# A macaron transformer block on one core: a first weight load in halves, five tiles' V copies on GpSimd, and the last block stored tile by tile from two queues

## The chip, the cores and the metric

The kernel runs on one core of a Trainium2 chip. The metric is the device time of one execution in microseconds (us); lower is better. The engines are named as in the profile: PE (TensorE matmuls), PEld (its weight loads), DVE (VectorE), ACT (ScalarE), POOL (GpSimd) and SP (SyncE, which here only issues DMAs). "SPq" and "ACTq" are the queues of SP and ACT, from which DMAs are issued.

## The reference, cut to what matters

The input is `x` of 2 x 2048 tokens with 256 features. The block is a feed-forward half, a local attention and a second feed-forward half with the same weights:

```python
x = x + 0.5 * ffn(layernorm(x))      # routed experts + shared expert
x = x + attn(layernorm(x))           # 16 heads of 16, causal within groups of 64 tokens
x = x + 0.5 * ffn(layernorm(x))

def ffn(x):                          # 4096 tokens x 256
    # top 2 of 8 experts, at most 640 tokens an expert, weights from a softmax
    routed = scatter_add(expert_e(tokens of e) * weight)     # expert: silu(x@rg) * (x@ru) @ rd, inner 1024
    shared = silu(x @ sg) * (x @ su) @ sd                    # inner 2048
    return shared + routed

def attn(x):                         # x: groups of 64 tokens
    q, k, v = split(x @ w_qkv); q, k = rmsnorm(q) * ln_w, rmsnorm(k) * ln_w
    return softmax(mask(q @ k.T / 4)) @ v @ w_proj
```

## The kernel before

Tokens are taken in 8 blocks of 512 (BT), a block in 4 tiles of 128 (P). Every fp32 operand of a large product is split into a high and a low fp16 part, and a product is three matmuls (`TERMS`: high x high, high x low, low x high). Four phases follow each other:

- **Phase a** normalises tiles, computes routing and runs the shared expert of blocks 0 to 3. The shared weights are loaded once at the start: `load_shared` (L124) goes over the 16 inner chunks in pairs, loads gate and up rows of a pair into a raw tile `rs` (tag `raw`, two DMAs), the down rows into `rd` (one DMA), and splits them into `sgu` and `sdw` (`split`, L104: ACT makes the high part, L107, DVE the low part, L109). The pair c = 0 is issued from ACT's queue, the others from SP's. The first product of the kernel, L398, waits for chunk 0 of `sgu`; it also needs the turned tiles `xb` (L200 to L202).
- **Phase b** runs the eight routed experts of the first half.
- **Phase c** runs the attention in 32 tiles (`attn_tile`, L625), beside the shared expert of the remaining blocks of the first half (4 to 7) and of the first seven blocks of the second half.
- **Phase d** runs the routed experts of the second half and then the shared expert of block 7, whose end is the end of the kernel.

The shared expert of a block (`shared`, L454) goes over 16 chunks c. `gate_up` (L385) makes gate and up in PSUM (tiles `pgu`, three buffers, 12 matmuls of 512 columns at L408), then SiLU (ACT L420; in phase c a tanh on ACT L416 and a DVE step L417 instead), the product with up (DVE L422), the high part `hh` (ACT L424) and the low part `hl` (DVE L425). `down` (L428) multiplies them with the down weights into two PSUM tiles `po` (12 matmuls of 256 columns, L435). It runs one chunk late: `defer` (L99) holds back a chunk's `down` until the next chunk's `gate_up` has been traced. In the very last chunk (block 7, c = 15) gate and up are made in two halves of 256 tokens, and `down` takes the tiles in pairs (0, 1) and (2, 3). Then `fin` adds the sums to the residual `xr` (DVE L472, one instruction for two tiles) and stores 256 KB at a time from SP (L475).

An attention tile projects q, k and v (`pqk` and `pv`, L768), splits v into `vs` (one buffer; ACT L658, DVE L659), normalises q and k (L651 to L664) and spreads them into `QK` (L674 to L681), transposes `QK` by DMA (L686), multiplies (`psc`, L694), adds the mask (DVE L697), takes the maximum (L703) and subtracts it (POOL L704). Then `vs` is copied into `V2`, a layout for pairs of heads: four copies of 64 x 512 fp16 (ACT L709). The exponential (ACT L713), its high part (ACT L715), its low part (POOL L716), a DMA transpose (L719), the product with V2 (`py`, L727), the division (L739 to L744) and the output projection (`pao`) follow. V2 has two buffers, taken in turn.

What order the instructions take on each engine is set when the program is built: the framework's scheduler issues, in a simulated time line, the instruction that comes first in the program's order among those that are ready. Two things bend that order: Python generators, which interleave the tracing of tiles with the tracing of chunks (`drive`, `run_slots`), and `tc.issue_after(ins)`, which puts what it encloses behind `ins` on that instruction's engine. On the chip every engine then runs its own list in order.

Of the kernel before, what the change touches and what calls it, by code (L numbers as in the profile page):

```python
# [15 lines left out]
ALU = mybir.AluOpType  # L16
# [4 lines left out]
P = 128  # L21
H = 256
# [3 lines left out]
WS = 16.0  # L26
XP = UP * WS
NB = 8
BT = 512
# [8 lines left out]
class Net:  # L38
# [85 lines left out]
    def load_shared(self, sg, su, sd):  # L124

        nc = self.nc
        w = self.wsh
        self.sgu = w.tile([P, 16, 2, 2, 2, P], F16, name="sgu")
        self.sdw = w.tile([P, 2, 16, H], F16, name="sdw")
        for c in range(0, 16, 2):  # L130
            issue = nc.sync if c else nc.scalar
            r = self.raw.tile([P, 2, 2, 2 * P], F32, name=f"rs{c}", tag="raw", bufs=4)
            for i, s in enumerate((sg, su)):
                issue.dma_start(
                    out=r[:, i], in_=s[:, c * P:(c + 2) * P].rearrange("(k p) f -> p k f", p=P))
            r2 = self.raw.tile([P, 2, H], F32, name=f"rd{c}", tag="raw2", bufs=4)
            issue.dma_start(out=r2, in_=sd[c * P:(c + 2) * P].rearrange("(k p) f -> p k f", p=P))
            if c == 0:
                yield
            for j in range(2):  # L140
                with self.behind(True, 0, 1, mark=self.turned[1] if c + j == 0 else None):
                    src = r[:, :, :, j * P:(j + 1) * P]
                    self.split(self.sgu[:, c + j, 0], self.sgu[:, c + j, 1], src, None if c + j else self.normal[3])
            with self.behind(True, 0, 1):
                self.split(self.sdw[:, 0, c:c + 2], self.sdw[:, 1, c:c + 2], r2)
            yield
# [238 lines left out]
    def gate_up(self, wc, x, h, tanh=False, first=False):  # L385


        nc = self.nc
        n = x.shape[-1]
        ps = []  # L390
        if first:
            ps = [self.ps_gu.tile([P, n], F32, name="pgu", tag="gu") for _ in range(2)]
            for half in range(2):
                t = slice(half * n // 2, (half + 1) * n // 2)
                for j, (w, a) in enumerate(TERMS):
                    for i in range(2):
                        for k in range(2):
                            nc.tensor.matmul(  # L398
                                ps[i][:, t], lhsT=wc[:, w, i, k, :], rhs=x[:, 2 * a + k, t],
                                start=(half == 0 and j + k == 0), stop=(half == 1 and j + k == 3),  # L400
                                skip_group_check=True)
        for i in range(2):
            if not first:
                p = self.ps_gu.tile([P, n], F32, name="pgu", tag="gu")
                j = 0
                for k in range(2):
                    for (w, a) in TERMS:
                        nc.tensor.matmul(  # L408
                            p, lhsT=wc[:, w, i, k, :], rhs=x[:, 2 * a + k, :], start=(j == 0), stop=(j == 5))
                        j += 1  # L410
                ps.append(p)
            p = ps[i]
            if i == 0:
                s = self.hp.tile([P, BT], F32, name="sl")[:, :n]
                if tanh:
                    nc.scalar.activation(s, p, AF.Tanh, scale=0.5 / XP)  # L416
                    nc.vector.scalar_tensor_tensor(  # L417
                        out=s, in0=s, scalar=1.0, in1=p, op0=ALU.add, op1=ALU.mult)
                else:
                    self.latest[0] = nc.scalar.activation(s, p, AF.Silu, scale=1.0 / XP).ins  # L420
                yield
        self.latest[1] = nc.vector.scalar_tensor_tensor(  # L422
            out=s, in0=ps[1], scalar=1.0 / XP / (2.0 * XP if tanh else 1.0), in1=s, op0=ALU.mult, op1=ALU.mult).ins
        self.highs.append(nc.scalar.copy(h[0], s).ins)  # L424
        self.lows.append(nc.vector.tensor_tensor(out=h[1], in0=s, in1=h[0], op=ALU.subtract).ins)  # L425
        yield
# [27 lines left out]
    def shared(self, b, xb, src, dst, tanh=False, late=2, last=False):  # L454
        nc = self.nc
        outs = [self.ps_out.tile([P, BT], F32, name="po", tag="po") for _ in range(2)]
        for c in range(16):
            if c == late:
                res = self.res_load(src, b)
            h = [a[:, 0:BT] for a in self.hbuf()]  # L460
            if last and c == 15:
                for t in (slice(0, BT // 2), slice(BT // 2, BT)):
                    yield from self.gate_up(self.sgu[:, c], xb[:, :, t], [a[:, t] for a in h], tanh)
            else:
                yield from self.gate_up(self.sgu[:, c], xb, h, tanh, b == 0 and c == 0 and not tanh)

            def fin(c=c, h=h):
                self.down(outs, 4, h, self.sdw[:, :, c], c, 16, last and c == 15)
                if c < 15:
                    return  # L470
                for i in range(2):
                    nc.vector.scalar_tensor_tensor(  # L472
                        out=res[i], in0=outs[i].rearrange("p (t f) -> p t f", f=H), scalar=0.5 / WS,
                        in1=res[i], op0=ALU.mult, op1=ALU.add)
                    nc.sync.dma_start(  # L475
                        out=dst[b * BT + i * 2 * P:b * BT + (i + 1) * 2 * P].rearrange("(t p) f -> p t f", p=P),
                        in_=res[i])

            self.defer(fin)
            yield  # L480
# [144 lines left out]
    def attn_tile(self, R, j, x2, new_fb):  # L625

        nc = self.nc
        a = self.at
# [12 lines left out]
        V2 = self.V2[j % 2]  # L641
# [8 lines left out]
        for i in range(2):  # L650
            nc.scalar.activation(qk[:, i, :], pqk[:, i, :], AF.Square, scale=1.0 / XP, accum_out=ss[:, i:i + 1])  # L651
        nc.vector.tensor_scalar(
            out=ss, in0=ss, scalar1=XP ** 2 / H, scalar2=1e-6 * XP ** 2, op0=ALU.mult, op1=ALU.add)
# [3 lines left out]
        vs = a.tile([P, 2, H], F16, name="vs")  # L657
        self.values = nc.scalar.mul(vs[:, 0, :], pv, 1.0 / XP).ins  # L658
        nc.vector.scalar_tensor_tensor(  # L659
            out=vs[:, 1, :], in0=pv, scalar=1.0 / XP, in1=vs[:, 0, :], op0=ALU.mult, op1=ALU.subtract)  # L660
        yield
        yield
        for i in range(2):
            nc.vector.scalar_tensor_tensor(  # L664
                out=qk[:, i, :], in0=pqk[:, i, :], scalar=ss[:, i:i + 1], in1=self.lnw,
                op0=ALU.mult, op1=ALU.mult)
        QS = self.QK[:, 0:16].rearrange("p (j s) (r a c) -> p j s r a c", s=2, r=2, a=4)
        for i in range(2):
            if i == 0:
                for r in range(2):  # L670
                    src = qk[:, 0, :].rearrange("p (j r c) -> p j r c", r=2, c=16)[:, :, r, :]
                    src = src.unsqueeze(2).to_broadcast([P, 8, 2, 16])
                    s = QS[:, :, r, r]
                    nc.scalar.copy(s[:, :, 0:2, :], src)  # L674
                    self.anchor = nc.gpsimd.tensor_tensor(
                        out=s[:, :, 2:4, :], in0=src, in1=s[:, :, 0:2, :], op=ALU.subtract)
            else:
                s = self.QK[:, 16:24].rearrange("p j (r a c) -> p (j r) a c", r=2, a=4)
# [3 lines left out]
                    out=s[:, :, 1::2, :], in0=src, in1=s[:, :, 0::2, :], op=ALU.subtract)  # L682
        yield
        QT = a.tile([P, 2, 24, 64], F16, name="QT")
        for g in range(2):
            nc.sync.dma_start_transpose(  # L686
                out=QT[:, g], in_=self.QK[g * 64:(g + 1) * 64].rearrange("p j c -> p (j c)"))
# [3 lines left out]
        for g in range(2):  # L691
            p = self.m1([P, 8, 64], F32, "psc")
            for jj in range(8):
                nc.tensor.matmul(  # L694
                    p[:, jj, :], lhsT=QT[:, g, 2 * jj:2 * jj + 2, :].rearrange("p r q -> p (r q)"),
                    rhs=QT[:, g, 16 + jj, :], start=True, stop=True)
            nc.vector.tensor_tensor(  # L697
                out=S[:, g * 8:(g + 1) * 8, :], in0=p,
                in1=self.mask.unsqueeze(1).to_broadcast([P, 8, 64]), op=ALU.add)
        yield  # L700
        mx = self.sm.tile([P, 16], F32, name="amx")
        with self.tc.issue_after(self.lows[-2]):
            nc.vector.tensor_reduce(out=mx, in_=S, axis=AX.X, op=ALU.max)  # L703
        self.anchor = nc.gpsimd.tensor_tensor(  # L704
            out=S, in0=S, in1=mx.unsqueeze(2).to_broadcast([P, 16, 64]), op=ALU.subtract)
        with self.tc.issue_after(self.highs[-2]) if j < 4 else nullcontext():
            for g in range(2):
                for d in range(2):
                    nc.scalar.copy(  # L709
                        V2[d * 64:(d + 1) * 64, g, :, :, 0:32].rearrange("p j l c -> p l j c"),  # L710
                        vs[g * 64:(g + 1) * 64].rearrange("p l (j c) -> p l j c", c=32))
        yield
        nc.scalar.activation(S, S, AF.Exp, scale=0.25)  # L713
        e16 = a.tile([P, 16, 2, 64], F16, name="e16")
# [9 lines left out]
        for g in range(2):  # L724
            py = self.m1([P, 512], F32, "py")
            for jj in range(7):
                nc.tensor.matmul(  # L727
                    py[:, jj * 66:(jj + 1) * 66], lhsT=ET[:, g * 8 + jj, :],
                    rhs=V2[:, g, jj].rearrange("p l c -> p (l c)")[:, 0:66], start=True, stop=True)
# [10 lines left out]
            for r in range(2):  # L740
                sl = slice(r * 64, (r + 1) * 64)
                c = slice(r * 16, (r + 1) * 16)
                nc.vector.tensor_tensor(out=Y[sl, g], in0=hi[sl, :, c], in1=yl[sl, :, c], op=ALU.add)
        nc.vector.tensor_tensor(  # L744
            out=Y, in0=Y, in1=rc.unsqueeze(3).to_broadcast([P, 2, 8, 16]), op=ALU.mult)
# [14 lines left out]
            po, lambda i, r: yt[:, r, 2 * i:2 * i + 2, :].rearrange("p g q -> p (g q)"), self.wpr, TERMS)  # L760
        nc.vector.scalar_tensor_tensor(out=y, in0=po, scalar=1.0 / WS, in1=y, op0=ALU.mult, op1=ALU.add)
        yield from self.front_steps(y, j % 4, new_fb, x2[j * P:(j + 1) * P])

    def project(self, ps, part, w, terms):
        i = 0
        for k in range(2):
            for (x, v) in terms:
                self.nc.tensor.matmul(ps, lhsT=part(x, k), rhs=w[:, v, k, :], start=(i == 0), stop=(i == 5))  # L768
                i += 1
# [234 lines left out]
```

## Time and profile before

| | |
|---|---|
| median of 3 runs | 1770.22 us (1770.21 to 1770.29) |
| the profiled execution's own time | 1770.79 us |
| its span in the trace | 1769.1 us |
| granted TensorE clock | 0.999 |
| PE busy | 1759.1 us (99%), 13229 matmuls |
| DVE, ACT, POOL busy | 1197.1, 956.8, 767.4 us |
| V copies (ACT L709) | 128, 617 ns median, first at 636.1 us |

The span is the time from the first to the last instruction of the core; the execution's time has 1.69 us more around it. All times of the trace are counted from the span's start. A matmul's end is modelled in the profile: a matmul of 512 columns is shown as 0.38 us long although the next one starts 0.216 us later, so a PE wait that the profile shows as idle time is shorter than what it costs by about 0.16 us.

### The profile page before, as it was taken

What the parts mean: (1) busy time and instruction counts of PE and PEld (TensorE: products, weight loads), DVE (VectorE), ACT (ScalarE), POOL (GpSimd) and SP (SyncE); (2) the same over time, 40 slices, a digit from 0 to 9 for tenths busy, and PEclk for the clock granted to TensorE, in tenths of its full rate; (3) what the DMA queues carried; (4) which work ended last, traced back from release to release, by engine and by line L of the source; (5) the groups of instructions that cost most, each with busy time, mean ns of one, the idle gap of its engine ahead of it and who ended that gap; (6) DMA issues with size and microseconds to landing.
All of it is one profiled execution on the core that took longest, in us unless ns stands there. A gap on an engine that the chain in (4) does not pass through costs nothing.

```text
span 1769.1 us, 36544 instructions
## 1 busy us (share of the span) xinstructions
PE 1759.1 (99%) x13229; PEld 1193.6 (67%) x13229; DVE 1197.1 (68%) x2874; ACT 956.8 (54%) x2119; POOL 767.4 (43%) x1123
## 2 busy tenths in 40 slices
PE   9999999999999999999999999999999999999998
PEld 6666667777777556666666666666665777777765
DVE  8756536666666667888788888888655566666643
ACT  5433335555555457676767667676332455555542
POOL 4777720221111435556777787776640011222210
PEclk9999999999999999999999999999999999999999
DMA  8444124555453254766676676765211145555420
GB/s 233 109 101 117 39 52 103 124 121 121 107 121 73 58 103 92 143 113 135 124 146 140 128 149 123 148 127 112 61 21 53 53 112 112 122 118 120 100 40 12
DMA packets 437542, 185.10 MB, mean 105 GB/s; under 512 B 302194, under 2 KB 434734, under 8 KB 437361
## 3 DMA queue, kind: packets, MB, share of 16 engines
q1 hardware_dynamic: 418592, 160.55, 40.9%
q0 software_dynamic: 17664, 21.17, 6.8%
q8 instruction: 103, 1.69, 0.4%
q10 hardware_dynamic: 1104, 1.05, 0.2%
q14 instruction: 79, 0.64, 0.1%
HBM read 78.16 MB, written 42.21 MB: 68 GB/s over the span
## 4 chain that ended last, share of the span: by engine, by line
PE 95%; DVE 2%; ACT 1%; issue 1%; DMA 1%; POOL 0%; ACTq 0%; POOLq 0%; DVEq 0%
PE pgu L408 59%; PE po L435 30%; PE pqk L768 2%; PE pao L768 1%; PE pv L768 1%; PE psc L694 1%; PE py L727 1%; DVE hl L425 0%; DVE sl L422 0%; DMA rs<-in_L_ffn_su_dram 0%; DVE sl L417 0%; ACT V L709 0%; DMA xt<-xa 0%; ACT hh L424 0%; PE pgu L398 0%
## 5 line engine op out<-in xcount | busy, mean ns | idle before, releaser
L408 PE MATMUL pgu<-xb,sgu 128*128 128x512 f16 x3072 | 721.1, 378 | 1.9 <-DVE sl L417 1.9
L424 ACT CAST hh<-sl 128x512 f16<-128x512 f32 (+2 forms) x513 | 273.5, 533 | 471.6 <-DVE sl L422 468.9
L408 PE MATMUL pgu<-xe,wc 128*128 128x384 f16 (+1 forms) x3072 | 497.7, 299 | 0.0
L408 PEld LDWEIGHTS <-sgu 128*128 128x128 f16 x3072 | 293.2, 98 | 283.9 <-issue 2.3
L422 DVE SCALAR_TENSOR_TENSOR sl<-pgu,sl 128x512 f32<-128x512 f32 (+2 forms) x513 | 301.7, 588 | 263.8 <-PE pgu L408 236.4
L425 DVE TENSOR_TENSOR hl<-sl,hh 128x512 f16<-128x512 f32 (+2 forms) x513 | 320.5, 625 | 149.5 <-ACT hh L424 148.1
L435 PEld LDWEIGHTS <-hh 128*128 128x128 f16 x3328 | 319.7, 98 | 88.2 <-ACT hh L424 2.1
L408 PEld LDWEIGHTS <-wc 128*128 128x128 f16 x3072 | 300.6, 98 | 91.7
L435 PE MATMUL po<-sdw,hh 128*128 128x256 f16 x2048 | 269.7, 272 | 0.7 <-ACT hh L424 0.7
L565 POOL DMA_INDIRECT out_dram<-eo,eidscatter x40 | 64.3, 1608 | 329.3 <-DVE eo L564 293.2
L420 ACT ACTIVATE sl<-pgu 128x384 f32<-128x384 f32 (+2 forms) x337 | 159.1, 472 | 73.0 <-PE pgu L408 49.9
L565 POOL DMA_INDIRECT acc<-eo,eidscatter x40 | 66.1, 1653 | 289.3 <-DVE eo L564 251.6
L435 PE MATMUL po<-wd,hh 128*128 128x256 f16 x1280 | 191.2, 273 | 0.0
L435 PEld LDWEIGHTS <-hl 128*128 128x128 f16 x1664 | 162.0, 98 | 34.7 <-DVE hl L425 2.3
L417 DVE SCALAR_TENSOR_TENSOR sl<-sl,pgu 128x512 f32<-128x512 f32 x176 | 119.7, 680 | 69.2 <-ACT sl L416 68.5
L376 POOL DMA_INDIRECT xg<-X,di x128 | 138.7, 1084 | 46.3 <-issue 22.3
L435 PE MATMUL po<-sdw,hl 128*128 128x256 f16 x1024 | 157.4, 273 | 0.5 <-DVE hl L425 0.4
L416 ACT ACTIVATE sl<-pgu 128x512 f32<-128x512 f32 x176 | 104.4, 593 | 43.0 <-PE pgu L408 38.9
L107 ACT ACTIVATE wc<-re 128x512 f16<-128x512 f32 x124 | 78.1, 630 | 72.9 <-PE pgu L408 72.9
L435 PE MATMUL po<-wd,hl 128*128 128x256 f16 x640 | 116.1, 273 | 0.0
L109 DVE SCALAR_TENSOR_TENSOR wc<-re,wc 128x512 f16<-128x512 f32 x124 | 85.6, 690 | 14.0 <-ACT wc L107 13.9
L709 ACT COPY V<-vs 64x512 f16<-64x512 f16 x128 | 79.0, 618 | 1.5
(165 smaller groups left out, 1745.1 us busy)
## 6 DMA issues: line engine op xcount, KB each, us to landing
re<-in_L_ffn_rg_dram SPq DMA_DIRECT2D x124, 128.0 KB, 2.3
re<-in_L_ffn_ru_dram SPq DMA_DIRECT2D x124, 128.0 KB, 2.7
re<-in_L_ffn_rd_dram SPq DMA_DIRECT2D x124, 128.0 KB, 2.6
y<-acc SPq DMA_DIRECT2D x64, 128.0 KB, 2.6
acc<-xr SPq DMA_DIRECT2D x16, 256.0 KB, 3.4
out_dram<-xr SPq DMA_DIRECT2D x16, 256.0 KB, 2.7
y<-in_L_attn_x_dram SPq DMA_DIRECT2D x30, 128.0 KB, 2.5
x<-y SPq DMA_DIRECT2D x28, 128.0 KB, 1.9
```

The source lines that it names most:

```text
L109: nc.vector.scalar_tensor_tensor(out=lo, in0=src, scalar=WS, in1=hi, op0=ALU.mult, op1=ALU.subtract)
L376: i = nc.gpsimd.indirect_dma_start(out=R["xg"][:, :], out_offset=bass.IndirectOffsetOnAxis(ap=di[:, t, k:k + 1], axis=0), in_=X, in_offset ...
L408: nc.tensor.matmul(p, lhsT=wc[:, w, i, k, :], rhs=x[:, 2 * a + k, :], start=(j == 0), stop=(j == 5))
L416: nc.scalar.activation(s, p, AF.Tanh, scale=0.5 / XP)
L417: nc.vector.scalar_tensor_tensor(out=s, in0=s, scalar=1.0, in1=p, op0=ALU.add, op1=ALU.mult)
L420: self.latest[0] = nc.scalar.activation(s, p, AF.Silu, scale=1.0 / XP).ins
L422: self.latest[1] = nc.vector.scalar_tensor_tensor(out=s, in0=ps[1], scalar=1.0 / XP / (2.0 * XP if tanh else 1.0), in1=s, op0=ALU.mult, op ...
L424: self.highs.append(nc.scalar.copy(h[0], s).ins)
L425: self.lows.append(nc.vector.tensor_tensor(out=h[1], in0=s, in1=h[0], op=ALU.subtract).ins)
L435: nc.tensor.matmul(outs[t // 2][:, (t % 2) * H:(t % 2 + 1) * H], lhsT=h[a][:, t * P:(t + 1) * P], rhs=wd[:, w], start=(c == 0 and j == 0 a ...
L565: i = nc.gpsimd.indirect_dma_start(out=R["acc"][:, :], out_offset=bass.IndirectOffsetOnAxis(ap=ids[:, t:t + 1], axis=0), in_=eo, in_offset ...
L709: nc.scalar.copy(V2[d * 64:(d + 1) * 64, g, :, :, 0:32].rearrange("p j l c -> p l j c"), vs[g * 64:(g + 1) * 64].rearrange("p l (j c) -> p ...
```

## The change

There are three edits.

1. In `load_shared` the gate and up loads of the pair c = 0 are made in two halves each: first the 128 columns of chunk 0 (gate, then up), then those of chunk 1. That is four DMAs of 128 KB in the place of two of 256 KB, with rows of 512 bytes in the place of 1024, from ACT's queue as before; the load of `rd` follows them.
2. In `attn_tile` the four V copies move into a function `spread`. For the tiles j = 0 to 4 they run on POOL, for the others on ACT as before. The `issue_after` that put the copies of tiles 0 to 3 behind a chunk's high part on ACT is gone.
3. In the last block `down` of chunk 14 is put behind `self.final`, the last gate/up matmul of chunk 15, and the four tiles' sums are formed and stored one by one: four DVE instructions of 128 x 256, and four stores of 128 KB, from SP (tiles 0 and 2) and ACT (tiles 1 and 3).

```diff
@@ load_shared
             r = self.raw.tile([P, 2, 2, 2 * P], F32, name=f"rs{c}", tag="raw", bufs=4)
-            for i, s in enumerate((sg, su)):
-                issue.dma_start(
-                    out=r[:, i], in_=s[:, c * P:(c + 2) * P].rearrange("(k p) f -> p k f", p=P))
+            for j in range(2 if c == 0 else 1):
+                f = slice(j * P, (j + 1) * P) if c == 0 else slice(0, 2 * P)
+                for i, s in enumerate((sg, su)):
+                    issue.dma_start(
+                        out=r[:, i, :, f], in_=s[:, c * P:(c + 2) * P][:, f].rearrange("(k p) f -> p k f", p=P))
@@ gate_up
-                        nc.tensor.matmul(
-                            p, lhsT=wc[:, w, i, k, :], rhs=x[:, 2 * a + k, :], start=(j == 0), stop=(j == 5))
+                        self.final = nc.tensor.matmul(
+                            p, lhsT=wc[:, w, i, k, :], rhs=x[:, 2 * a + k, :], start=(j == 0), stop=(j == 5)).ins
@@ shared, fin
-                self.down(outs, 4, h, self.sdw[:, :, c], c, 16, last and c == 15)
+                with self.tc.issue_after(self.final) if last and c == 14 else nullcontext():
+                    self.down(outs, 4, h, self.sdw[:, :, c], c, 16, last and c == 15)
                 if c < 15:
                     return
-                for i in range(2):
+                for t in range(4 if last else 0):
+                    r = res[t // 2][:, t % 2]
+                    nc.vector.scalar_tensor_tensor(
+                        out=r, in0=outs[t // 2][:, (t % 2) * H:(t % 2 + 1) * H], scalar=0.5 / WS,
+                        in1=r, op0=ALU.mult, op1=ALU.add)
+                    (nc.scalar if t % 2 else nc.sync).dma_start(out=dst[b * BT + t * P:b * BT + (t + 1) * P], in_=r)
+                for i in range(0 if last else 2):
@@ attn_tile
-        with self.tc.issue_after(self.highs[-2]) if j < 4 else nullcontext():
-            for g in range(2):
-                for d in range(2):
-                    nc.scalar.copy(
-                        V2[d * 64:(d + 1) * 64, g, :, :, 0:32].rearrange("p j l c -> p l j c"),
-                        vs[g * 64:(g + 1) * 64].rearrange("p l (j c) -> p l j c", c=32))
+        for g in range(2):
+            self.spread(V2, vs, g, j < 5)
@@ new
+    def spread(self, V2, vs, g, pool):
+
+        for d in range(2):
+            (self.nc.gpsimd.tensor_copy if pool else self.nc.scalar.copy)(
+                V2[d * 64:(d + 1) * 64, g, :, :, 0:32].rearrange("p j l c -> p l j c"),
+                vs[g * 64:(g + 1) * 64].rearrange("p l (j c) -> p l j c", c=32))
```

## The prediction

> **What bounds the kernel now.** I read the page first (busy time, chain), then the windows by stage to find where PE is idle, then PE's waits, and the timeline at each place.
>
> ```profile
> PE 95%; DVE 2%; ACT 1%; issue 1%; DMA 1%; POOL 0%; ACTq 0%; POOLq 0%; DVEq 0%
> ```
>
> The chain of work that ended last is PE. No edit removes a matmul, so only time in which PE waits can be won. The windows (start:end, length, then busy time of PE, PEld, DVE, ACT, POOL, clock, DMA share, GB/s) show where that is:
>
> ```profile
> 0.00:10.00 10.00, 7.80 (x75) 7.00 (x76) 5.59 (x22) 3.20 (x7) 6.31 (x36) 1.00 0.79 250
> 640.00:660.00 20.00, 18.73 (x142) 11.26 (x141) 13.23 (x23) 12.15 (x24) 8.86 (x8) 1.00 0.68 131
> 660.00:680.00 20.00, 19.39 (x145) 11.81 (x145) 16.50 (x28) 13.88 (x28) 9.37 (x9) 1.00 0.68 109
> 680.00:700.00 20.00, 19.82 (x151) 12.06 (x149) 15.94 (x40) 13.95 (x33) 9.89 (x11) 1.00 0.54 99
> 700.00:720.00 20.00, 18.87 (x149) 11.71 (x147) 17.03 (x36) 14.69 (x32) 10.06 (x10) 1.00 0.57 97
> 720.00:1240.00 520.00, 520.00 (x4130) 329.59 (x4129) 427.79 (x1095) 362.99 (x797) 377.00 (x514) 1.00 0.67 132
> ```
>
> PE is idle at the start (2.20 us of the first 10), in the first 80 us of the attention (1.27 + 0.61 + 0.18 + 1.13 = 3.19 us), not at all from 720 to 1240, and at the end. The three edits stand at these three places. All of it is under 10 us of 1770, so the question is a few us; 0.2%, about what a measurement of this kernel can tell from no change, is 3.5 us.
>
> **Edit 1, the first weights.** In the timelines of ACT and PE, in brackets the idle time before an instruction and what ended it:
>
> ```profile
> 8.28 0.63 ACT L107 ACTIVATE sgu<-rs 128x512 f16<-128x512 f32 x1 [0.70 <-DMA rs<-in_L_ffn_su_dram]
> 8.97 1.05 PE L398 MATMUL pgu<-xb,sgu 128*128 128x256 f16 x8 [0.67 <-ACT sgu L107]
> ```
>
> The chain of the first 16 us has "2.27 5.93 DMA rs<-in_L_ffn_su_dram": up's load, issued at 2.27, lands at 8.20. ACT had ended its second turned tile (L201, 7.21 + 0.37) at 7.58 and waited 0.70. Chunk 0 now needs half of the 512 KB; in place of 8.20, I take the landing of gate's whole load, the first half of the same bytes, which the trace's semaphore has at 7.33. I add 0.15 for the shorter rows (the traced packets of 512 bytes take 27 ns, those of 1024 bytes 46) and get 7.5. Then ACT starts at 7.6, since the tile of 7.58 is ahead of it: 0.68 earlier. PE could then start at 8.29. What it needs next is ready: the low part of turned tile 1 at 8.04, the third tile's transpose at 8.30. Before the low part of the weights (L109, 9.11) DVE has z of tile 3 at 8.32 to 8.73, so it can move forward only to about 8.9, and the low-part matmuls follow the transposes and logits anyway. From 10 to 600 us PE is never idle, so an earlier start is kept. The two added issues cost ACT's queue two times about 0.4 us (0.39 and 0.49 for L134) and push `rd` back by 0.8; its split runs at 11.07, and the second chunk's at 10.54, well behind. **-0.65 us**, between -0.9 and 0 (nothing if the slowest DMA engine is as late as now).
>
> **Edit 2, the V copies.** Twenty copies leave ACT: 20 x 0.617 = 12.3 us, which matters only where PE waits behind them. Two of PE's largest waits:
>
> ```profile
> 656.08 2.50 ACT L709 COPY V<-vs 64x512 f16<-64x512 f16 x4
> 658.60 0.60 ACT L416 ACTIVATE sl<-pgu 128x512 f32<-128x512 f32 x1
> ...
> 698.55 1.25 ACT L709 COPY V<-vs 64x512 f16<-64x512 f16 x2
> 699.82 1.06 ACT L713 ACTIVATE S<-S 128x1024 f32<-128x1024 f32 x1
> 700.79 0.58 ACT L416 ACTIVATE sl<-pgu 128x512 f32<-128x512 f32 x1
> ```
>
> Each time the tanh (L416) is late behind copies, then L417 on DVE, and PE waits for a PSUM buffer. The timeline has PE idle 0.36 us before 659.98 and 0.92 before 702.14, both "<-DVE sl L417". From start to start of the matmuls the gaps are 0.51 and 1.06 over the normal step, since a matmul's modelled end overlaps the next; a third one at 674.97, behind the copies at 670.94 to 673.44, has 0.24. Sum 1.81 us, and the copies (2.5 us a tile) are longer than each of the waits, so they should go whole. The other waits in the stage have other causes: hh late at 648.46 behind L178, which waits for the transpose of xa, and after it L417 at 650.80 (0.45 + 0.75), and POOL holding DVE up (below). They stay.
>
> The price is on POOL. A copy of 64 x 512 fp16 on POOL is not in the trace. Nearest rows: 64 x 64 fp32 0.23 us (L591, 1 input, an eighth of the size); 128 x 512 with two inputs 1.16 (L681, median of the undisturbed). Half of L681's part for its two inputs and the fixed 0.2 gives about 0.7; I take 0.8, ends 0.4 and 1.16. The Trainium skill (GPSIMD Engine Reference, section 3.1) has 769 ns for 512 elements of a one-input loop; by it the 20 copies are an estimate of 15.4 us. With 0.8 they are 16 us in about 85 us in which POOL is busy for half (8.86 to 10.06 of 20). The copies can issue as soon as `vs` is written (L659), and only the product with V2, some 15 us later, needs them, so POOL's own lateness is covered. What is queued behind them is POOL's chain of an attention tile (L654, L704, L716), late by at most one or two copies. `vs` and the PSUM tile `pv` come free sooner: L658 of tile 2 stood at 659.10, right behind tile 1's copies.
>
> The cost that reaches PE goes through DVE:
>
> ```profile
> 679.23 2.13 POOL L716 TENSOR_TENSOR e<-S,e 128x1024 f16<-128x1024 f32 x1 [2.59 <-ACT e L715]
> 680.42 1.49 DVE L425 TENSOR_TENSOR hl<-sl,hh 128x512 f16<-128x512 f32 x1 [0.68 <-ACT hh L424]
> ```
>
> L425 takes 0.69 undisturbed; here it ended 0.55 after POOL did. Between 600 and 725 us the 25 L425 take 21.4 us in the place of 17.3, so POOL costs them 4.1, and L744 (1.80 for 0.41) another 1.4. DVE instructions that read PSUM (L417, L422) do not stretch beside POOL. Of the 5.5 us, 1.4 reached PE (0.35, 0.34 and, by way of L744, L652, L654 and L664, 0.70): a quarter. The Trainium skill (SBUF — State Buffer, "SBUF: two separate sides") says that a DVE operation with two SBUF inputs and a GpSimd operation lock each other out for a whole instruction, which speaks against this edit; by that rule, the trace agrees (1.49 for 0.69). With the copies on POOL for 16 of 85 us, some 4 of 20 chunks' L425 meet one and lose half a copy or more, about 2 us of DVE's time in all, and a quarter of it is **+0.5 us** on PE (ends 0 and 7, below). Edit 2 in sum: -1.81 + 0.5 = **-1.3 us**.
>
> **Edit 3, the end.**
>
> ```profile
> 1763.82 0.61 PE L435 MATMUL po<-sdw,hh 128*128 128x256 f16 x4 [0.37 <-ACT hh L424]
> 1764.57 0.39 PE L435 MATMUL po<-sdw,hl 128*128 128x256 f16 x2
> 1764.99 0.69 DVE L472 SCALAR_TENSOR_TENSOR xr<-po,xr 128x512 f32<-128x512 f32 x1 [0.49 <-PE po L435]
> ```
>
> The last pair of tiles waits for hh and hl of the second half, which end at 1763.77 and 1764.50 because the last gate/up (6 matmuls at 1761.97) runs after chunk 14's `down` (12 matmuls at 0.109 = 1.31 us). Swapped, the last gate/up starts at 1760.66, L422 follows by 1761.6, hh by 1762.5, hl by 1762.95. `down` 14 and the first pair fill PE until 1763.29, then the last six run without a wait and end at 1764.11, where they now end at 1764.96. PSUM has room: the last gate/up tile takes the buffer that L420 leaves at 1760.00. DVE then forms tile 0 at 1763.48 and the rest back to back, 4 x 0.42 (L422's 128 x 256 row): the last sum ends at 1765.15 in the place of 1765.68, **-0.53**. The final store carries 128 KB in the place of 256; the DMA view has the stores at 330 GB/s, so 0.39 us less, and ACT's queue is empty: **-0.39**. From that store to the span's end nothing changes. Edit 3: **-0.9 us** (-0.5 to -1.2).
>
> **Sum.** -0.65 - 1.3 - 0.9 = -2.85. The profiled execution is 1769.1 + 1.69 = 1770.79, which gives 1767.9; the median is 0.57 below it: 1770.22 - 2.85 = **1767.3 us** (-0.16%). Within 0.2%: chance 0.51.
>
> **Rivals.**
> - *The attention's start loses all its waits.* `vs` and `pv` come free up to 15 us sooner, ACT has 12 us more room, and the list is scheduled anew, so the remaining waits (start to start some 4.5 us in 600 to 725, of which I took 1.81) could go too. Against it: those behind the xa transpose and L716 have other causes. Time: -0.65 - 0.9 - 4.5 = -6.05, 1764.2. Half of it is enough to pass 0.2%. Chance 0.35 for everything faster than -3.5.
> - *Two of the edits do nothing:* the first half lands no sooner, because the slowest DMA engine sets it, and POOL's blocking eats what ACT gives. Only the end remains: 1769.3. Chance 0.09.
> - *POOL's copies stall DVE (slower).* If each of the 20 copies takes the upper 1.16 us and stops an L425 or L744, and each reaches PE like the 0.35 of 681.97, that is +7.0: -0.65 - 1.81 - 0.9 + 7.0 = +3.6, 1773.9. It decides from about 10 of the 20 on. Against it: 25 L425 met some 40 us of POOL's work and only three waits came of it. Chance 0.05.
>
> So faster 0.35, within 0.2% 0.51 + 0.09 = 0.60, slower 0.05. The range leaves out the last rival and the fastest part of the first: 1764.0 to 1770.0; the likeliest case alone has 1766.7 to 1769.
>
> **What would show it.** L107's first instruction at about 7.6 and L398 at 8.3; 20 copies on POOL at 0.8 us and 108 on ACT; PE's waits on L417 down from 1.9 us to about 0.6, and PE idle from 640 to 720 under 2 us; L425's mean there not above 0.9; no PE wait in the last 6 us, four sums of 0.42 and the last store issued 0.5 us earlier against the last matmul's old place. Wrong if L107 stays at 8.28, if PE's idle time after 640 is as before or L425 stretches past 1 us on average.

## The result and the profile after

The changed kernel takes 1764.95 us (median; 1764.86 to 1765.52) against 1770.22 before: -5.27 us, a ratio of 0.9971 with a 95% interval of 0.9962 to 0.9980. The forecast was 1767.3 with a range of 1764.0 to 1770.0. The time lies in the range, but 2.35 us below the forecast, and -0.30% is beyond the 0.2% within which I had put most of the chance.

To see where the time went, I compare the traces at equal work. Each matmul counts with the time that its columns take; at a given sum of such work, the two traces' times are subtracted. "100 us of work" is the point at which PE has done 100 us of matmuls.

| stage | forecast | first trace after | second (on another chip) |
|---|---|---|---|
| start to 100 us of work | -0.65 | +0.49 | +0.20 |
| 600 to 720 us of work | -1.81 | -4.95 | -4.94 |
| 720 to 1220 us of work | +0.5 (POOL's price, wherever) | +0.39 | +0.38 |
| 1220 us of work to the last matmul | -0.85 | -0.85 | -0.85 |
| last matmul to the end | -0.05 | -0.44 | -0.42 |
| sum (rounded) | -2.85 | -5.36 | -5.63 |

So edit 1 did not pay at all, edit 2 paid far more than I had it pay, and edit 3 a little more. The span goes from 1769.1 to 1763.7. The chain of the whole span after, by engine:

```profile
PE 99%; DMA 1%; DVE 0%; issue 0%; ACTq 0%; DVEq 0%; ACT 0%
```

DVE's 2% and ACT's 1% of before are gone from it. The windows after (start:end, length, busy time of PE, PEld, DVE, ACT, POOL, clock, DMA share, GB/s) show the start and the attention:

```profile
0.00:10.00 10.00, 7.13 (x75) 6.46 (x76) 5.82 (x23) 3.79 (x9) 6.51 (x36) 1.00 0.77 231
640.00:660.00 20.00, 20.00 (x151) 12.23 (x149) 16.41 (x27) 12.49 (x24) 10.98 (x9) 1.00 0.70 133
660.00:680.00 20.00, 20.00 (x157) 12.77 (x155) 16.62 (x30) 11.48 (x25) 12.55 (x16) 1.00 0.68 113
680.00:700.00 20.00, 20.00 (x153) 12.49 (x152) 17.31 (x39) 12.09 (x30) 14.11 (x16) 1.00 0.44 86
700.00:720.00 20.00, 20.00 (x159) 12.69 (x157) 17.34 (x38) 13.26 (x29) 10.85 (x11) 1.00 0.60 117
```

PE is busy all of 640 to 720, where it had 3.19 us of idle time, and it gets 620 matmuls done there in the place of 587. In the first 10 us it is busy for less (7.13 against 7.80).

**The start.** ACT's timeline after, then PE's:

```profile
6.07 0.46 ACTq L139 DMA_DIRECT2D rd<-in_L_ffn_sd_dram  x1
...
7.72 0.62 ACT L107 ACTIVATE sgu<-rs 128x512 f16<-128x512 f32 x1
...
12.30 0.63 ACT L107 ACTIVATE sdw<-rd 128x512 f16<-128x512 f32 x1 [2.02 <-DMA rd<-in_L_ffn_sd_dram]
```

```profile
8.57 0.77 PE L202 MATMUL ptx<-ident,z 128*128 128x128 f32 x4 [0.97 <-DVE xb L204]
9.18 1.04 PE L400 MATMUL pgu<-xb,sgu 128*128 128x256 f16 x8
```

(Lines behind `load_shared` are two higher than before: L400 was L398.) L107 starts at 7.72, close to the 7.6 of the forecast. But the lists have changed. Two lines of DVE after, then three of DVE and PE before:

```profile
7.77 0.41 DVE L172 TENSOR_SCALAR z<-y,mv,rstd 128x256 f32<-128x256 f32 x1 [0.66 <-POOL rstd L158]
8.10 0.75 DVE L204 TENSOR_TENSOR xb<-ptx,xb 128x256 f16<-128x256 f32 x2
```

```profile
7.20 0.39 DVE L202 TENSOR_TENSOR xb<-ptx,xb 128x256 f16<-128x256 f32 x1
7.86 0.44 PE L200 MATMUL ptx<-ident,z 128*128 128x128 f32 x2
9.85 0.38 PE L200 MATMUL ptx<-ident,z 128*128 128x128 f32 x2
```

On DVE the fourth tile's `z`, which waits for POOL, now stands ahead of the low parts of the first two turned tiles, so these start at 8.10 in the place of 7.20. On PE the third tile's transposes (7.86 before) wait for the low parts, and the fourth tile's (9.85 before, behind the first gate/up) now stand ahead of the first gate/up. It starts at 9.18, later than the 8.97 of before. And `rd`, issued at 3.59 before, is issued at 6.07 and lands at 12.28. The chain of the first 16 us shows what it waits for:

```profile
1.84 4.20 DMA rs<-in_L_ffn_sg_dram
6.05 0.02 issue
6.07 6.21 DMA rd<-in_L_ffn_sd_dram
```

The issue of `rd` follows the landing of the first gate half. The loads take eight completion counters in turn (by the numbers in the trace), and in ACT's list `rd` now waits, before it is issued, for the counter of an earlier load, as do the two loads that the edit adds.

**The attention.** All instructions of the V copies after, by engine (ns: least, median, most):

```profile
L772 ACT COPY V<-vs x108: 615/617/622, 710.9 to 1215.1; 64x512 f16<-64x512 f16 x108
L772 POOL COPY V<-vs x20: 600/612/1071, 619.9 to 698.0; 64x512 f16<-64x512 f16 x20
```

And two groups of 600 to 725 us (busy, mean ns | idle before, by releaser), after and then before:

```profile
L427 DVE TENSOR_TENSOR hl<-sl,hh 128x512 f16<-128x512 f32 x27 | 23.5, 871 | 8.9 <-ACT hh L426 8.6
L418 ACT ACTIVATE sl<-pgu 128x512 f32<-128x512 f32 x27 | 16.0, 591 | 19.9 <-PE pgu L410 18.2 <-PE pl L245 1.7
```

```profile
L425 DVE TENSOR_TENSOR hl<-sl,hh 128x512 f16<-128x512 f32 x25 | 21.4, 856 | 15.9 <-ACT hh L424 15.7
L416 ACT ACTIVATE sl<-pgu 128x512 f32<-128x512 f32 x26 | 15.4, 593 | 3.9 <-PE pgu L408 3.8
```

DVE's low part still stretches (871 ns mean, 856 before), so POOL holds it up as much as it did. But the tanh on ACT, which waited for its matmuls for 3.8 us in this stretch before, waits for 18.2 now: it is early where it had been late. PE's waits between 600 and 725 us were these before (us in total, times, longest), and none is left after:

```profile
PE pgu L408 <- DVE sl L417: 1.9, 3, 0.9
PE psc L694 <- DVE qk L664: 0.5, 1, 0.5
PE po L435 <- DVE hl L425: 0.4, 2, 0.2
PE po L435 <- ACT hh L424: 0.3, 1, 0.3
```

**The end.** The timeline after, all engines:

```profile
1759.42 1.42 DVE L476 SCALAR_TENSOR_TENSOR xr<-po,xr 128x256 f32<-128x256 f32 x4 [0.58 <-PE po L437]
...
1759.65 0.38 PE L437 MATMUL po<-sdw,hl 128*128 128x256 f16 x2
1759.87 1.02 SPq L479 DMA_DIRECT2D out_dram<-xr  x2
1760.20 1.03 ACTq L479 DMA_DIRECT2D out_dram<-xr  x2
```

The six last matmuls run without a wait, and the four sums overlap: 1.42 us for four, where four times 0.42 would be 1.68.

### The profile page after: what moved, and what is told of

Its sections match the earlier page's. It is cut to its first block, busy times and chain, and to the rows that moved or that the text cites. A ratio compares the mean times of both kernels' runs of the same rounds, so it can differ in the third digit from the quotient of the medians.

```text
span 1763.7 us, 36544 instructions
## 1 busy us (share of the span) xinstructions
PE 1756.5 (100%) x13229; PEld 1193.5 (68%) x13229; DVE 1199.8 (68%) x2876; ACT 945.8 (54%) x2099; POOL 778.7 (44%) x1143
## 3 DMA queue, kind: packets, MB, share of 16 engines
q10 hardware_dynamic: 1936, 1.31, 0.2%
## 4 chain that ended last, share of the span: by engine, by line
PE 99%; DMA 1%; DVE 0%; issue 0%; ACTq 0%; DVEq 0%; ACT 0%
PE pgu L410 61%; PE po L437 31%; PE pqk L780 2%; PE pao L780 1%; PE pv L780 1%; PE psc L703 1%; PE py L732 1%; DMA rd<-in_L_ffn_sd_dram 0%; DMA rs<-in_L_ffn_sg_dram 0%; PE py L737 0%; PE pl L245 0%; PE pl L243 0%; DVE xr L481 0%; PE pp L286 0%; ACTq L814 0%
## 5 line engine op out<-in xcount | busy, mean ns | idle before, releaser
L427 DVE TENSOR_TENSOR hl<-sl,hh 128x512 f16<-128x512 f32 (+2 forms) x513 | 320.4, 625 | 143.3 <-ACT hh L426 141.8
L107 ACT ACTIVATE wc<-re 128x512 f16<-128x512 f32 x124 | 78.0, 629 | 73.1 <-PE pgu L410 73.1
L721 POOL TENSOR_TENSOR e<-S,e 128x1024 f16<-128x1024 f32 x32 | 68.3, 2133 | 16.8 <-ACT e L720 16.6
```

What stands on the lines that cost most here:

```text
L107: nc.scalar.mul(hi, src, WS)
```

## The experiments

### Each edit alone, and two together

In each, only the named part of the change's diff is in; the rest is the kernel before. They ran on one chip, on which the kernel before takes 1771.43 us.

```diff
@@ load_shared (first kernel: this alone)
+            for j in range(2 if c == 0 else 1):
...
@@ attn_tile (second kernel: this alone)
+        for g in range(2):
+            self.spread(V2, vs, g, j < 5)
...
@@ shared, fin (third kernel: this alone; fourth kernel: this and the second)
+                with self.tc.issue_after(self.final) if last and c == 14 else nullcontext():
...
```

Edit 1 alone. 

> Edit 1 alone (first load in halves). Theory, from the changed kernel's trace: it costs, since the down weights of the first pair are issued at 6.07 (a DMA counter is still held by the first half) and land at 12.28, and ACT and PE wait for them; +0.5 us, 1770.7. The prediction had -0.65, 1769.6. A third view, that its shift of the schedule is what emptied the attention's start of waits, would make it 3 us or more faster, 1767 or less.

Edit 2 alone. 

> Edit 2 alone (V copies of five tiles on POOL). Theory: all waits of PE between 600 and 720 us go by this edit: -4.9 there, some 0.4 given back later, so -4.5, 1765.7. The prediction's sum (only waits behind copies go, POOL's lock costs 0.5) has -1.3, 1768.9. If the gain needs another edit's shift of the schedule: between -1 and -3.

Edit 3 alone. 

> Edit 3 alone (last chunk's order and four stores). Theory from the changed trace: last matmul 0.85 earlier, last store 0.27 shorter, 0.24 less from its landing to the end: -1.3, 1768.9. The prediction had -0.9, 1769.3. A rival, that part of it is luck of the new list, has -0.5 or less.

Edits 2 and 3. 

> Edits 2 and 3 without edit 1. If the three edits add up and edit 1 costs 0.5: 0.5 faster than all three, 1764.4. If edit 1 gives what was predicted (-0.65): 1765.6. If the schedule of the attention depends on edit 1: 1766 or more.

| edits | time, us | ratio (95%) | 600 to 720 us of work | end (last 30 us of work on) |
|---|---|---|---|---|
| 1 | 1772.35 | 1.0004 (0.9995 to 1.0013) | +0.5 | -0.1 |
| 2 | 1767.19 | 0.9975 (0.9965 to 0.9986) | -4.94 | 0 |
| 3 | 1769.75 | 0.9992 (0.9983 to 1.0001) | 0 | -1.17 |
| 2 and 3 | 1766.47 | 0.9970 (0.9959 to 0.9981) | -4.95 | -1.17 |

The medians differ from before by +0.92, -4.24 and -1.68: together -5.0, about the whole change. Edit 2 carries it. These sums hold to about 1 us only: edits 2 and 3 in one kernel give -4.96, where their two differences add up to -5.92. From 550 to 800 us the kernels with edit 1 or edit 3 alone have the order of before on all four engines, so the new order there comes with edit 2. Edit 1 alone has the start of the change's trace, with the four transposes first and the first gate/up at 9.54. By themselves the intervals of edits 1 and 3 hold 1.

The traces also show that one profiled start is not enough. Ten traces of this study have the first loads of before and, on all four engines, its order at the start (the kernel before, and nine runs without edit 1). L107 starts in them between 7.23 and 8.28 us, and before's profile, from which I predicted, is the latest of the ten. PE's first gate/up starts 0.68 to 0.74 us after L107 in each, 8.41 on average (7.92 to 8.97). The three traces with edit 1 as it is have it at 9.18, 9.22 and 9.54. At 100 us of work they are 0.34 us behind before's profile on average (0.20 to 0.49), the ten 0.5 ahead of it (0 to 0.94): by the starts, edit 1 costs some 0.9 us.

### Is it that `vs` comes free early, or that ACT's copies are no longer put behind a chunk?

Two kernels leave the copies on ACT. They and the two kernels of the next part shared a chip with 1770.43 us before.

```diff
-        vs = a.tile([P, 2, H], F16, name="vs")
+        vs = a.tile([P, 2, H], F16, name="vs", bufs=2)
```

> The kernel before with two buffers for vs in the place of one; the V copies stay on ACT, behind the same high part. It frees vs and pv early without taking work from ACT. Early freeing theory: PE's wait time between 600 and 720 us falls by most of edit 2's 4.9, so 4 to 5 us faster than before. ACT time theory (what counts is 2.5 us of copies a tile in ACT's list): under 1 us. New list alone: anything between -2 and +2.

```diff
-        with self.tc.issue_after(self.highs[-2]) if j < 4 else nullcontext():
+        with nullcontext():
```

> The kernel before without the issue_after that held the copies of tiles 0 to 3 behind a chunk's high part; they stay on ACT and are listed as soon as vs is there. Early freeing theory: vs comes free at once, so 3 to 5 us faster, though ACT has the same work. ACT time theory: no gain, or slower by up to 2, since copies now stand ahead of tanh and high part.

Two buffers of `vs`: 1769.47 us, 0.9993 (0.9984 to 1.0003); 600 to 720 us of work gained 1.3 us of the 4.95. Without `issue_after`: 1771.61, 1.0007 (0.9997 to 1.0016); the stretch lost 0.4. PE's waits from 600 to 745 us of that kernel (us in total, times, longest):

```profile
PE po L435 <- ACT hh L424: 1.6, 1, 1.6
PE psc L694 <- DVE vs L659: 0.9, 1, 0.9
```

The waits have moved from one step of the chunk to another. So neither part alone makes the gain, and the kernel that frees `vs` early has about a quarter of it. Both kernels also have an order of their own in this stretch, which the comparison can't take out.

### POOL's copies, later or doubled

```diff
+        for g in range(2):
+            with self.tc.issue_after(self.anchor.ins):      # behind the same tile's L704 on POOL
+                self.spread(V2, vs, g, j < 5)
```

> Edit 2 alone, but the POOL copies of tiles 0 to 4 are listed behind the same tile's subtraction on POOL (L704 of before), so vs and pv are held as long as before while ACT is relieved as in the change. ACT time theory: the whole 4.9 us between 600 and 720, 4 us or more faster than before. Early freeing theory: only the three waits right behind copies go (1.8), 1 to 2 us faster.

```diff
+        for d in (0, 1, 0, 1) if pool else (0, 1):
```

> Edit 2 alone with every POOL copy made twice (40 in the place of 20, the second pair writes the same values again). It doubles the suspected price on POOL and of the lock against DVE. Prediction's price: 0.5 us more than edit 2 alone in 600 to 720. Slower rival (0.35 for each copy): 7 us more. If POOL's slack covers it: under 0.3.

Late copies hold `vs` longer than even ACT's did: the second to fifth tile's L658 stands at 648.78, 667.60, 684.93 and 706.04, where before has 639.13, 659.10, 673.96 and 694.79, and edit 2 alone 631.19, 642.52, 664.18 and 683.80. Even so the stretch of 600 to 720 us of work gained 4.9 us, the whole of it. Doubled copies gained about 4.1, some 0.8 less than edit 2 alone: near the 0.5 of the prediction's price and far from the 7 of the slower rival, but it is one wait, at 673.38 us, for ACT's high part and not for DVE's low part. Both kernels are slower all the same: 1775.21 us, 1.0026 (1.0015 to 1.0036), and 1779.52, 1.0052 (1.0035 to 1.0068). They lost some 10 and 12 us between 720 and 800 us of work, where no POOL copy runs any more. PE's waits from 725 to 900 us, first the two largest of the late copies, then all of the doubled ones:

```profile
PE pl L241 <- DMA xb<-X: 2.6, 1, 2.6
PE psc L694 <- DVE y L758: 1.2, 1, 1.2
```

```profile
PE py L723 <- DMA ET<-e: 4.4, 2, 4.1
PE pqk L771 <- DMA xt<-xa: 2.5, 1, 2.5
```

The waits are not all of the loss. After the three longest of them (2.6, 2.5 and 4.1 us) the trace shows PE at half its clock for a while; the third number from the end is the granted clock, first for the late copies, then twice for the doubled ones:

```profile
785.00:787.80 2.80, 2.80 (x14) 1.40 (x11) 1.38 (x4) 0.69 (x2) 0.48 (x1) 0.50 0.22 46
```

```profile
773.60:777.20 3.60, 3.60 (x11) 1.34 (x10) 2.97 (x19) 0.84 (x4) 0.99 (x2) 0.53 0.44 103
819.50:824.90 5.40, 5.40 (x32) 2.83 (x33) 3.29 (x10) 4.71 (x9) 3.24 (x4) 0.50 0.99 224
```

Matmuls of 512 columns start 0.427 us apart there in the place of 0.216. That costs 1.4 us of the 10, and 1.7 and 2.6 us of the 12. The 1.6 us of wait in the kernel without `issue_after`, above, had no such stretch behind it.

None of the longest waits is for a POOL copy itself. Both kernels have, from the first attention tiles on, another order of instructions than edit 2 alone, and in it PE reaches products whose transposes by DMA have not landed. It isn't excluded that the copies hand their own lateness on along the tiles: the sixth tile's L658 stands at 730.2 and 729.5 us, with edit 2 alone at 702.0. Either way a kernel can lose 10 us in a place where the edit has no instruction, twice what the whole change gains.

### ACT's time put back; the whole change again, without edit 1, and with `rd` on SP's queue

These four ran on one chip (1770.06 us before). In the first, POOL makes the copies of tiles 0 to 4 as in edit 2, and ACT makes the same copies once more into a tile that nobody reads, so that it has its 12.3 us to do again.

```diff
+            if j < 5:
+                spare = a.tile([P, 2, 8, 2, 34], F16, name="spare")
+                with self.tc.issue_after(self.highs[-2]):
+                    for g in range(2):
+                        self.spread(spare, vs, g, False)
```

> Edit 2 with ACT's time put back: POOL makes the copies of tiles 0 to 4, and ACT makes the same four copies of each of these tiles a second time into a spare tile that nobody reads, behind a chunk's high part as in the kernel before. Theory (PE's waits went because ACT has 12.3 us more room): the waits of 600 to 720 us come back, 3 to 5 us of the 4.95, and the kernel is within 1.5 us of the kernel before. Rival (vs and the product with V2 are free sooner because POOL copies at once): vs is held as long as before here too, since the spare copies read it, so this rival expects the same 3 to 5 us; the two are told apart with the kernel that frees vs early and leaves the copies on ACT, which gained 1.3. Rival (another list has fewer waits by luck): 600 to 720 us gains 4 us or more as with edit 2 alone.

It takes 1768.51 us, 0.9992 (0.9983 to 1.0002). By the sum the waits came back: of 4.94 us that edit 2 alone gains from 600 to 740 us of work, 1.36 are left. By their place and cause they did not. Up to 680 us of work this kernel has gained 4.2 us, edit 2 alone 4.4, though ACT did its copies:

```profile
L768 POOL COPY V<-vs 64x512 f16<-64x512 f16 x20 | 14.3, 715 | 0.8
L768 ACT COPY spare<-vs 64x512 f16<-64x512 f16 x20 | 12.3, 616 | 0.2
```

At the third tile the tanh stands right behind four copies here too, and PE does not wait: it has 18 gate/up matmuls to do meanwhile.

```profile
665.99 4.05 PE L408 MATMUL pgu<-xb,sgu 128*128 128x512 f16 x18
666.46 2.50 ACT L768 COPY spare<-vs 64x512 f16<-64x512 f16 x4
668.98 0.60 ACT L416 ACTIVATE sl<-pgu 128x512 f32<-128x512 f32 x1
```

What it loses comes later, and none of it is a chunk's step that is late on ACT. PE's timeline from 700 us on, with its waits alone:

```profile
701.89 0.18 PE L241 MATMUL pl<-rwt,xb 128*128 128x16 f16 x1 [0.68 <-DMA xb<-X]
...
713.11 0.39 PE L728 MATMUL py<-V,ET 128*128 128x66 f16 x7 [0.73 <-DMA ET<-e]
...
729.08 0.39 PE L728 MATMUL py<-V,ET 128*128 128x66 f16 x7 [0.38 <-DMA ET<-e]
```

The exponential of the fourth tile runs at 702.25 us here and at 694.29 with edit 2 alone; its transpose, and the product behind it, are late. So the waits behind copies went without ACT's relief: up to there it isn't what removes them. Whether the late exponential is the price of ACT's copies or of the order, this run doesn't tell: ACT is idle for 2.27 us before its high part at 696.96, and for 1.10 us before L178 at 698.68. Nor does `vs` come free much sooner here (L658 at 637.64, 656.07, 670.22 and 690.35). This kernel too has a list of its own, which the comparison can't take out.

The whole change again. 

> The whole change again, on the same chip as the three runs beside it. All theories: 5.3 us below the kernel before (4.5 to 6.0), and in the trace the same three places as the first time: equal work reached 0 to 0.5 us later than before at 100 us (a start that costs), 4.9 us gained between 600 and 720 us, 1.2 us at the end. How much of the gain is lost again between 720 and 1220 us (PE's waits on hl L427, 0.3 us in the first trace, 0.3 to 1.5 in the kernels with edit 2 alone or 2 and 3) differs from run to run if it is chance, and stays at 0.3 if it belongs to this list.

It takes 1764.97 us, 0.9973 (0.9963 to 0.9983), and its trace is the last column of the first table. All three places came out as the first time, and the loss between 720 and 1220 us too (0.38 after 0.39).

Edits 2 and 3 again. 

> Edits 2 and 3 without edit 1, beside the whole change on the same chip. If edit 1 costs 0.9 us at the start, as the traces of the starts say, this kernel is 0.5 to 1.3 us faster than the whole change. If the starts differ by chance alone, the two are equal within 0.5. If edit 1 pays 0.65 as the prediction had it, this kernel is 0.65 us slower.

1764.56 us, 0.9969 (0.9958 to 0.9980): 0.41 below the whole change on the same chip, less than I expected from the starts, and a difference that the intervals don't separate. In the traces it is 1.03 ahead in the span (1762.4 against 1763.4), all of it made in the first 20 us. Its PE starts so:

```profile
7.62 0.44 PE L200 MATMUL ptx<-ident,z 128*128 128x128 f32 x2
7.92 1.05 PE L398 MATMUL pgu<-xb,sgu 128*128 128x256 f16 x8
```

`rd` from SP's queue, all three edits in:

```diff
-            issue.dma_start(out=r2, in_=sd[c * P:(c + 2) * P].rearrange("(k p) f -> p k f", p=P))
+            nc.sync.dma_start(out=r2, in_=sd[c * P:(c + 2) * P].rearrange("(k p) f -> p k f", p=P))
```

> All three edits, and the first down rows rd are issued from SP's queue in the place of ACT's, so that they no longer wait for a DMA counter behind the first gate half. Theory (edit 1 loses at the start because rd is issued 2.5 us late and four transposes stand ahead of the first gate/up): rd lands before 10 us in the place of 12.28, the wait of 2.02 us on ACT at 12.3 and PE's gap behind it at 13.05 are gone, and PE is 0.5 to 1.0 us ahead of the whole change at 100 us: 0.5 to 1.0 us faster than it. Rival (the order of PE's first instructions alone does it, or the starts differ by chance): under 0.3 us of difference.

1766.42 us, 0.9979 (0.9970 to 0.9988): 1.45 slower than the whole change beside it. The first part of the theory held: `rd` is issued at 1.71, ACT splits it at 10.49 without a wait, and PE's first gate/up starts at 8.56. The wait came back elsewhere. The gate load of the second pair is now issued at 4.33 and its up load at 7.18, against 3.45 and 4.14, and by 40 us of work all that was won and more is lost, at

```profile
32.40 0.18 PE L243 MATMUL pl<-rwt,xb 128*128 128x16 f16 x1 [0.59 <-DMA xb<-X]
```

At 100 us of work it is 0.4 behind the whole change on its chip. It lost another 1.25 us near 727 us to the transpose of `e`, although its four engines have the very order of the whole change from 550 to 800 us.

## Why the prediction was right or wrong

The time lies in the range, but not by the sum that was written down: in the traces edit 2 gave 3.1 us more than its -1.81, and edit 1 cost where it was to gain. That the two misses partly cancel is luck, and the range reaches down to 1764.0 only because it takes in the first rival.

**Edit 1: wrong in sign (-0.65 forecast; about +0.9 by the starts; +0.41 and +0.92 by the medians, within their intervals).** The failing step is "PE could then start at 8.29. What it needs next is ready." I kept the lists as they were and asked only when data would be there. The build made others: two tiles' transposes stand ahead of the first gate/up in the place of one, and they wait for low parts that DVE now makes 0.9 us later. A smaller miss of the same step: the two added issues were to "push `rd` back by 0.8"; it was 2.5 us, since I counted the queue's time and not what the issue waits for. And the 0.70 us of ACT's wait that the edit was to remove was there in one profile: in seven of the ten traces with before's loads ACT waits there for less than 0.1 us. The 7.33 was misread too: it is the landing of the third tile's `y`, and gate's whole load landed at 7.52. The half does land earlier than I put it (6.05 for gate, 6.47 for up); it is not what decides.

**Edit 2: the right place and sign, mis-sized, and the mechanism not confirmed.** The term "1.81 us" is the one that failed: I credited only waits with a copy directly ahead of the late tanh, and wrote of the others "They stay". All of them went, 4.9 us, in the five traces whose engines have one and the same order from 550 to 800 us (edit 2 alone, edits 2 and 3 twice, the change twice); the kernel with `rd` on SP's queue has that order too and kept 3.7 of them. That a tanh behind four copies makes PE wait, as I read it, isn't so by itself either: with the spare copies it stood there and PE did not wait. The first rival had all of the waits go, with -4.5 for this stage; its time, 1764.2, is 0.75 from the one measured, partly since its miss on edit 1 cancels what it missed at the end.

Of the three reasons that the rival gave, the experiments speak for the last, the new list, by elimination only. Early freeing of `vs` came with 1.3 us and isn't needed (late POOL copies hold it longer than before). ACT's 12 us aren't needed for the waits up to 680 us of work. Taking `issue_after` away from ACT's copies gives nothing. What the kernels without these waits have in common is that POOL fills V2 and that the list was made anew with it; in those with V2's copies on ACT, whose order is that of before or nearer to it, the waits stay or move. What exactly in the new order does it I could not isolate: each of these edits in the attention changes the order of all four engines around it. That stays open.

**The price of POOL's copies, +0.5.** In the stage itself it is nil. The mechanism is there: in the trace after, an L427 at 658.27 took 1.31 us for 0.69 and ended 0.55 after POOL's L713, and the POOL copy behind it took 1.07 for 0.61. The Trainium skill (SBUF — State Buffer, "SBUF: two separate sides") describes such a lock in both directions; by that rule, the trace agrees. But DVE's delays meet slack now. The copy cost 0.61 us undisturbed and 0.67 on average, not 0.8. The Trainium skill (GPSIMD Engine Reference, section 3.1) gives 769 ns for a one-input loop of this length; the trace has a fifth less, and decides. The 0.39 us lost between 720 and 1220 us of work lie behind the last POOL copy. Kernels with the same list lost between 0 and 2.1 there, by waits for the low part, and the list of before 0 to 1.0. The losses go with the chip more than with the edit: the four kernels of the first experiments, all on one chip, lost 0.9 to 2.1, the other traces with these two lists 0 to 0.7. On that one chip the two kernels with edit 2 lost 1.1 more than the two without it, so a price of the edit isn't excluded.

**Edit 3: right, a little small (-0.9 forecast, -1.29 in the trace).** The last matmul is 0.85 us earlier, exactly as worked out, and no wait is left in the last 6 us. Two terms were off. The last sum ends 0.77 earlier, not 0.53, since the four sums overlap. From the last store's landing to the end there are 0.96 us left in the place of 1.20, where I had "nothing changes". At the end SP goes through the completion counters in a fixed order, 0.06 us each: before, five instructions of it follow the one that waits for the last store, after, one. Which counter the last store gets follows from the loads and stores ahead of it, and I hadn't looked: with edit 3 alone three follow, and with edit 1 alone too, which is its 0.1 us in the table. Against that the smaller store saves 0.27 and not 0.39.

**The signs that I named.** L107 at 7.6: yes. The first gate/up at 8.3: no, 9.18. Twenty copies on POOL and 108 on ACT: yes. PE's waits on L417 down to 0.6: they went to 0. PE idle under 2 us from 640 to 720: none at all. L425's mean not above 0.9: 0.871 (0.89 to 0.91 in the other traces of this order). Four sums of 0.42: they overlap, as said. The slower rival (POOL stalls DVE) had no part in it; the two kernels that came out clearly slower lost most by waits for DMA and the slow stretches behind them.

**The chances.** I had 0.35 on a gain beyond 0.2% and 0.60 on none. The profile had spoken for more: the windows showed 3.19 us of idle PE in one place, and an edit that moves twenty instructions there has the whole of it made anew. I treated each wait as bound to its own cause.

The fastest kernel measured is the one with edits 2 and 3 alone (0.9969); whether it beats the change by 0.4 us is not settled by these runs.

## What to carry to other kernels

Where a scheduler writes the lists, an edit's price is not the sum of its instructions: compare two traces at equal work, stage by stage, and compare the engines' orders before giving a cause to a wait. A wait of half a microsecond at the start of one profile may be that run's alone, so look at the same place in every trace that shares the code. And a load added ahead of others can hold back the issue of a later one by microseconds, so ask what each issue waits for as well as how long the queue takes for it. Where PE has waited for a few microseconds, look at the granted clock behind the wait: the wait alone was not the whole loss here.

## What the runs showed that I had not expected

- The same first loads end, and L107 starts, anywhere from 7.23 to 8.28 us after the span's start: a spread of 1.05 us from one profiled execution to the next with the same order of instructions. At 100 us of work the ten traces still differ by 0.94.
- After a wait of 2.5 to 4.1 us, PE's granted clock was 0.50 to 0.53 for some 3 to 5.5 us, which cost another 1.4 to 2.6 us each time.
- With the same order on every engine from 550 to 800 us, PE waited 1.1 us for the transpose of `e` in one trace and not at all in five. The transpose was issued at 721.68 there, and at 720.89 and 720.77 in the two traces of the whole change.
- DVE sums of 128 x 256 out of PSUM, 0.42 us alone, start 0.33 to 0.34 us apart when they follow each other.
